# A two-layer graph network on one core: three more products of the second half cut into an inner seven, and the order of the work around them changed

## The chip, the cores and the metric

The kernel runs on one core of a Trainium2 chip. The metric is the device time of one execution, in microseconds (us). The engines named are PE (TensorE, the matrix multiplier, with PEld for its weight loads), DVE (VectorE), ACT (ScalarE), POOL (GpSimd) and SP (which issues transfers). Matmuls write to PSUM[...]; the other engines take results out of the banks ("evict" below) to SBUF. POOL doesn't read PSUM here: it adds and subtracts blocks that lie in SBUF.

## What is computed

The reference, cut to what matters. `x` is 16 x 1024 x 64, `adj` is 1024 x 1024, all in float32.

```python
# layer 0, attention over the nodes, then a residual and a layernorm
score = softmax(einsum('bnc,bmc->bnm', Q, K), axis=1)
out = einsum('bnm,bmc->bnc', einsum('bnm,mc->bnc', score, adj), V)
x = layernorm(x + out)
# layer 1, two hops over the graph (both supports are adj), then a residual and a layernorm
x1 = adj @ x0;  x2 = 2.0 * (adj @ x1) - x0        # twice, with the same adj
out = concatenate([x0, x1, x2, x1, x2], -1) @ weight + bias
x = layernorm(x + out)
```

The kernel applies the weights before the hops, so that layer 1 becomes a chain of products of `adj` with a 1024 x 1024 matrix (nodes by 8 pairs of batches with 2 x 64 channels each): first z = B + adj · Y, then the output = X + adj · z. Y, B and X are three mixtures of x0.

## The kernel before, in words

Nodes lie on the partitions: a tile [128, 8, 1024] holds a 1024 x 1024 matrix. `aT` holds adj transposed, `UY` holds Y, `XB` holds B and then z, `xs` holds X and then the output. Columns are ordered by pair p = 0 to 7; the "second half" is pairs 4 to 7, columns 512 to 1023.

Every large product is done as Strassen-Winograd's seven products over 2 x 2 blocks. `SIDE[1..7]` are the seven left operands: four blocks of adj (1, 2, 4, 7; `SIDE[1]` and `SIDE[2]` lie in `aT` itself) and three sums of blocks (3, 5, 6, in `S`). The right operands are four blocks and four sums of blocks. Each product is added to one to three of the four result blocks (`TO`): 1 and 2 to 00, 5 and 7 to 11, 6 to 01, 10 and 11, 4 to 10, 3 to 01. In the order `STEPS` = 1, 2, 7, 5, 6, 4, 3 the products 6, 4 and 3 are accumulated in PSUM on top of the bank that still holds 1, 7 and 5 (`CHAIN`). So 6 can't start before 1 has been evicted, 4 not before 7, and 3 not before 5.

A main loop over the eight pairs does attention; products of the first layers fill the gaps of PE. Its last matmul ends 430.43 us into the span. Behind it stands the tail, which is written out by hand: the order in the program is the order on each engine, and the change is made there. The tail does the rest of z's second half, then the product adj · z with an inner seven in each of its seven products (`one` to `seven`), then the last layernorm and the stores.

A product of z's second half has a left operand of 512 x 512 and a right one of 512 x 256. It can be done in two ways:

- direct, in two steps g = 0 and 1 (`z_step(n, g)`), each of 8 matmuls of 256 columns (16 instructions, since one float32 matmul is recorded as two), one bank, and DVE adds of 128x512 to each place it goes to, at L658;
- by an inner seven (`Inner`, `of_z(n, sa, tb)`): the product is cut again. Four sums of blocks of the left side (`of_a`, into `sa`, 128x512 each) and four of the right side (`of_b`, into `tb`, 128x256 each) are made at L727, by POOL unless DVE is named. The seven steps have 4 matmuls of 128 columns each (8 instructions), and their evictions are 128x256. Step 7 needs `sa[2]` and `tb[2]`, step 5 `sa[0]` and `tb[0]`, step 6 `sa[1]` and `tb[1]`, step 4 `tb[3]`, step 3 `sa[3]`. Steps 1 and 2 need no sums.

Before the change, products 3 and 4 of z's second half (called z3 and z4 here) have an inner seven; 1, 2, 5, 6 and 7 are direct. The four sums of the right operands at the outer level, 128x1024 each, are made by DVE at L238 (`hop_z.sums(k)`): sums(1) makes operand 5, sums(2) operand 6, sums(3) operand 7, sums(4) operand 4.

The last pair, q = 7, also ends its attention in the tail: `values` (PE), adds on DVE, `squared` (ACT), `spread` (DVE, and a power on POOL, L424), `normed` and a transpose (DVE), two transfers to turn the layout (SP), a copy into order on ACT (`x0T_in_order`), and then `mix(q, kk)` for kk = 0, 2, 4, 6: PE makes two nodes' rows of the three mixtures in two banks, ACT evicts Y and B (L465, L466), then DVE evicts X (L470). `mix(6, kk)` are the last of pair 6. `added(U, 0, 0)` are two transfers issued on POOL's queue that add U, a result of `one`, to `xs`; they wait for `one`'s last evictions. What POOL has to do later is queued behind them.

The sums need scratch. Tiles are taken by tag (`xT`, `GT`, `o`, `t`, `oT`, `u`, `e`), and a new tile of a tag waits until the old one's readers are done. z3's and z4's left sums lie before the change in V (the second result tile of `one`'s kind) and in tiles `xT`.

Of the kernel before, what the change touches and what calls it, by code (L numbers as in the profile page):

```python
# [11 lines left out]
ALU = mybir.AluOpType  # L12
# [14 lines left out]
def gnn_kernel(  # L27
# [156 lines left out]
    def quarter(big_tile, h, r, c):  # L184

        t = big_tile[:, K4 * r : K4 * (r + 1), h * H + c * Q : h * H + (c + 1) * Q]
        return t.rearrange("p k (q f) -> p q k f", q=2)
# [97 lines left out]
    def xT(p):  # L285
        if p not in XT:
            XT[p] = att.tile([P, N], FP, tag="xT", name="xT")
        return XT[p]
# [243 lines left out]
    y = [[quarter(UY, 0, r, c) for c in range(2)] for r in range(2)]  # L532
    hop_z = Hop(lambda r, c: y[r][c], into(XB, 0), (y[0][1], y[1][1], y[0][0], y[1][0]), u, THIRD)
    runs = []
    for hop, orders in (
        (hop_0, (((6, 7), ONE), ((5, 3), ONE))),
        (hop_1, (((1, 2), ONE), ((6, 7, 4), ONE), ((5, 3), ONE))),
        (hop_z, (((1, 2), ONE), ((5, 3), ONE), ((6, 7, 4), ONE))),
    ):
        runs += [(hop, n, g) for order, groups in orders for g in groups for n in order]  # L540
    more = {(0, 1), (0, 3), (HP + 1, 3), (HP + 2, 3), (NP - 1, 2), (NP - 1, 3)}


    ahead, behind_all = {}, {
        (0, 0): [lambda: transposed(1, xT(1))], (0, 3): [value_weights], (0, 4): [mix_weights],
        (1, 0): [lambda: hop_1.sums(1)], (1, 5): [lambda: hop_1.sums(2)],
        (2, 0): [lambda: hop_1.sums(4)],
        (HP + 2, 5): [lambda: hop_z.sums(2)], (HP + 2, 6): [lambda: hop_z.sums(3)],
        (HP + 2, 7): [lambda: hop_z.sums(4)],
    }  # L550
    ahead.update({
        (0, 1): [lambda: sums_of_adj(1)], (0, 2): [lambda: sums_of_adj(4)],
        (2, 0): [lambda: hop_1.sums(3)], (HP + 1, 4): [lambda: hop_z.sums(1)],
    })

    def later(step, do, p):
        behind_all.setdefault(step, []).append(lambda: do(p))

    for p in range(NP):
        later((p, 4 if p else 5), means, p)  # L560
        later((p, 6) if p != HP + 2 else (p + 1, 0), centre, p)
        if p + 1 < NP:
            later((p + 1, 1), spread, p)
            later((p + 1, 2), normed, p)
            later((p + 1, 3), x0T, p)
        if p + 2 < NP:
            later((p, 7), lambda p: transposed(p, xT(p)), p + 2)
    mix_of = {(p, m): (p - 1, 2 * (m - 5)) for p in range(1, NP) for m in (5, 6, 7)}
    mix_of.update({(p, 1): (p - 2, K8 - 2) for p in range(2, NP)})

    for m in (6, 7):
        del mix_of[NP - 1, m]

    def run():

        hop, n, group = runs.pop(0)
        po = f_tile(f"p{n}")
        hop.product(po, n, group, True)
        return lambda: hop.evict(po, n, group)

    late, late_too = [run() for _ in range(2)], []
    for p in range(NP):
        q = p - 1
        for m in range(K8):
            nxt = (p, m + 1) if m + 1 < K8 else (p + 1, 0)
            if nxt[0] < NP:
                sc = scores(*nxt)
            scaled(p, m)
            for evict in late:
                evict()  # L590
            late = []
            for do in ahead.get((p, m), ()):
                do()
            if m == 1 and p:
                squared(q)
            if m == 5 and p:
                x0T_in_order(q)
            behind = late_too + [run()]
            late_too = []
            weighted(p, m)  # L600
            if nxt[0] < NP:
                exps(*nxt, sc)
            for evict in behind:
                evict()
            for do in behind_all.get((p, m), ()):
                do()
            if m == K8 - 1:
                attended(p)
            if (p, m) in more:
                (late_too if m == 1 else late).append(run())  # L610
            if m == 0 and p:
                late += values(q)
            if m == 2 and p + 1 < NP:
                late.append(project(p + 1))
            if (p, m) in mix_of:
                late += mix(*mix_of[p, m])
    assert not runs

    for evict in late:
        evict()
# [4 lines left out]
    q = NP - 1  # L629
    for_pool, for_vector = [], []  # L630

    def behind(pool=2, vector=1):

        for _ in range(min(vector, len(for_vector))):
            for_vector.pop(0)()
        for _ in range(min(pool, len(for_pool))):
            for_pool.pop(0)()
# [25 lines left out]
    hop_z = Hop(lambda r, c: y1[r][c], None, t, None, None)  # L663
# [4 lines left out]
    def z_step(n, g, **kw):  # L668
        step(
            held[CHAIN.get(n, n), g], n, SIDE[n][:, :, ts(g, 2 * P)], hop_z.side[n],  # L670
            lambda r, c: d_z(r, c, (2 * g, 2 * g + 1)), to=TO_Z,
        )
        behind(**kw)
# [68 lines left out]
    def of_z(n, sa, tb):  # L742

        return Inner(n, lambda r, c: hop_z.side[n][:, c, 2 * r : 2 * r + 2], sa, tb)
# [6 lines left out]

    def own(c):

        t = [att.tile([P, 2, K4, P], FP, tag="e", name=f"own{c}", bufs=4) for c in range(2)]
        return t, lambda r, c: t[c][:, :, 2 * r : 2 * r + 2].rearrange("p q g f -> p g q f")
# [75 lines left out]
    X, Y = ("xT", "xT", "GT", "GT"), ("o", "t", "oT", "u")  # L831
    one = of_full(1, X)
    (a3, a2, a1, a4), of_b = one.of_a, one.of_b
    for_vector += one.sums((a3, *of_b[:3], a2, a1, of_b[3], a4), nc.vector)
    for evict in mix(q - 1, 2):
        evict()
    z_step(2, 0, vector=2)
    for evict in values(q, w[1:3]):
        evict()
    squared(q)  # L840
    z_step(1, 0, vector=2)
    for evict in mix(q - 1, K8 - 4):
        evict()
    spread(q)
    z_step(2, 1, vector=2)
    for evict in mix(q - 1, K8 - 2):
        evict()
    normed(q)
    x0T(q)
    for do in for_vector:  # L850
        do()
    for_vector.clear()
    U, d_u = own(0)
    for i, n in enumerate(STEPS):
        one.step(n, w, d_u, True)
        behind()
        if i == 4:
            x0T_in_order(q)
    for kk, banks in (0, None), (2, (w[1], w[0])):
        for evict in mix(q, kk, banks):  # L860
            evict()
    hop_z.sums(1)

    V, d_v = own(1)
    t = [v.rearrange("p q k f -> p (q k f)") for v in V]
    z3 = of_z(
        3, blocks_of(t, Q),
        [SIDE[1][:, k, 0:Q].rearrange("p (k f) -> p k f", k=2) for k in range(K4)],
    )
    t = tiles(*X[:3])  # L870
    z4 = of_z(4, blocks_of(t[:2], Q), blocks_of(t[2:], P))
    for do in added(U, 0, 0) + z3.sums(z3.of_a) + z4.sums(z4.of_a):
        do()
    z_step(1, 1)
    for evict in mix(q, K8 - 4):
        evict()
    z_step(5, 0)
    for evict in mix(q, K8 - 2):
        evict()
    hop_z.sums(2)  # L880
    z_step(5, 1)
    hop_z.sums(3, 4)
    two = of_full(2, Y)
    for do in (
        z3.sums(z3.of_b) + z4.sums(z4.of_b) + two.sums(two.of_a) + two.sums(two.of_b)
    ):
        do()
    for g in range(2):
        for n in (6, 7):
            z_step(n, g)  # L890


    turn = [f_tile(f"w{i}") for i in (4, 5)] + [w[i] for i in (1, 0, 3, 2)]
# [6 lines left out]
    for z_n, d in (z3, in_z(0, 1)), (z4, in_z(1, 0)):  # L900
        b4 = next_banks(4)
        for n in STEPS:
            z_n.step(n, b4, d)


    five = of_full(5, X)
# [3 lines left out]
    for i, n in enumerate(STEPS):  # L910
        two.step(n, b4, in_x(0, 0))
        behind()
        if i == 1:
            (a3, a2, a1, a4), of_b = five.of_a, five.of_b
            for do in five.sums((a3, *of_b[:3], a2, a1, of_b[3], a4)):
                do()
    six = of_full(6, Y)
# [4 lines left out]
    for i, n in enumerate(STEPS):  # L922
        five.step(n, b4, d_v, True)
        behind()
        if i in (0, 2, 4):
            (norm.square, norm.variance, norm.out)[i // 2]()
    seven = of_full(7, X)
# [3 lines left out]
    for n in STEPS:  # L931
        six.step(n, b4, d_u)
        behind()
# [5 lines left out]
    for i, n in enumerate(STEPS):  # L939
        seven.step(n, b4, d_w, True)  # L940
        if i == 1:
            for_pool += added(V, 1, 1) + added(V, 0, 1)
        behind(4)
        if i in (0, 2, 4):
            (norm.square, norm.variance, norm.out)[i // 2]()
# [90 lines left out]
```

## Time and profile before

| | us |
|---|---|
| median of three runs | 582.42 (582.37 to 583.14) |
| the profiled execution, whole | 582.48 |
| its span, from first to last instruction | 580.6 |
| first matmul of the tail | at 430.43 |
| z's second half done (first step of `two`) | at 497.69 |
| `seven` done (first of the wide steps, L951) | at 546.12 |

| window (us) | PE busy | DVE busy | ACT busy | POOL busy |
|---|---|---|---|---|
| 430 to 440 | 10.00 | 3.89 | 2.76 | 0.00 |
| 440 to 450 | 10.00 | 9.11 | 2.16 | 2.90 |
| 450 to 460 | 10.00 | 4.70 | 4.18 | 2.94 |
| 460 to 470 | 10.00 | 6.15 | 1.57 | 9.69 |
| 470 to 480 | 10.00 | 8.35 | 0.00 | 9.69 |
| 480 to 490 | 10.00 | 4.93 | 0.00 | 9.67 |
| 490 to 500 | 10.00 | 5.61 | 0.00 | 1.27 |

A row of the second table gives the time in which each engine had an instruction under way. In a timeline line of the profile the numbers are the start, the time until the group's last end, the engine, the line of the program, the operation, the tile written and those read, the shape, and the count; in brackets stands the idle time before it and what ended it. Durations of neighbours overlap by some 0.05 to 0.1 us, so the distance between two starts is used where one follows another.

### The profile page before, as it was taken

Reading aid. Unit: us, or ns where it says so; the run is one execution under the profiler, and the core shown is the slowest. Engines: PE = TensorE matmul, PEld = TensorE weight load, DVE = VectorE, ACT = ScalarE, POOL = GpSimd, SP = SyncE. Lnnn points to the kernel's source line nnn. Section 1 sums busy time; section 2 is a strip of 40 time slices with the busy share of each in tenths; the row PEclk is TensorE's granted clock in tenths of the full one; section 3 lists DMA queues with packets and bytes.
Section 4 is the critical chain, followed back from the end, with each engine's and each line's share of the span. In section 5 each row is a group of like instructions: output and inputs, shape, how many; then the busy total and the mean of one; then the engine's idle time right before and its main releaser. Section 6 shows DMA issues by size and latency. Waiting matters only on the chain.

```text
span 580.6 us, 9494 instructions
## 1 busy us (share of the span) xinstructions
PE 571.9 (99%) x3774; PEld 328.7 (57%) x3774; DVE 441.1 (76%) x725; ACT 243.9 (42%) x517; POOL 113.9 (20%) x75
## 2 busy tenths in 40 slices
PE   8999999999999999999999999999999999999995
PEld 7754545444444444444444454444458889988744
DVE  0788878878867887787787777888858575689776
ACT  1134344556546545555554544554532300023471
POOL 0000002000200100100010010001001497494785
PEclk9999999999999999999999999999999999999999
DMA  8901001202022020211202011000200600001955
GB/s 258 337 21 53 1 26 49 72 1 74 1 73 73 2 73 2 73 40 35 73 1 73 37 37 71 4 1 2 72 1 1 146 0 2 2 0 37 173 134 164
DMA packets 26350, 33.35 MB, mean 57 GB/s; under 512 B 3010, under 2 KB 19650, under 8 KB 25922
## 3 DMA queue, kind: packets, MB, share of 16 engines
q1 hardware_dynamic: 24130, 28.55, 14.7%
q0 software_dynamic: 2176, 4.19, 4.0%
q8 instruction: 30, 0.49, 0.4%
q14 instruction: 14, 0.11, 0.1%
HBM read 16.48 MB, written 12.06 MB: 49 GB/s over the span
## 4 chain that ended last, share of the span: by engine, by line
PE 95%; DVE 1%; DMA 1%; SPq 1%; ACT 1%; POOL 0%; issue 0%; POOLq 0%; ACTq 0%
PE p L246 23%; PE sc L354 21%; PE acc L390 19%; PE w L643 16%; PE pm L455 5%; PE w L951 3%; PE wide L643 2%; PE pq L323 1%; PE po L407 1%; PE pv L246 1%; PE pu L246 1%; DMA early<-in_wqT_dram 1%; SPq L91 0%; DVE xs L799 0%; DVE var L421 0%; ACT xs L805 0%
## 5 line engine op out<-in xcount | busy, mean ns | idle before, releaser
L368 ACT ACTIVATE e<-sc,nm 128x1024 f32<-128x1024 f32 x128 | 142.7, 1115 | 150.8 <-DVE nm L366 150.8
L366 DVE TENSOR_REDUCE nm<-sc 128x1 f32<-128x1024 f32 x128 | 150.7, 1219 | 43.1 <-PE sc L354 42.9
L424 POOL TENSOR_TENSOR rstd<-var,expo 128x16 f32<-128x16 f32 (+3 forms) x21 | 50.7, 2420 | 429.9 <-DVE ri L376 377.1
L354 PE MATMUL sc<-xT,GT 64*128 64x512 f32 x512 | 126.8, 605 | 0.0
L390 PE MATMUL acc<-e,us 128*64 128x512 f32 x512 | 120.7, 592 | 0.0
L354 PEld LDWEIGHTS sc<-xT,GT 64*128 64x128 f32 x512 | 51.6, 186 | 49.2 <-issue 37.7
L390 PEld LDWEIGHTS acc<-e,us 128*64 128x64 f32 x512 | 36.7, 137 | 45.8 <-issue 36.6
L470 DVE TENSOR_TENSOR xs<-pm,bias 128x128 f32<-128x128 f32 x62 | 17.8, 290 | 19.3 <-ACT XB L466 17.8
L455 PEld LDWEIGHTS pm<-w,x0T_k 64*128 64x128 f32 x248 | 19.4, 186 | 22.8 <-DVE UY L267 6.5
L246 PE MATMUL p<-XB,S 128*64 128x256 f32 x256 | 31.1, 385 | 0.0
L246 PE MATMUL p<-UY,aT 128*64 128x256 f32 x256 | 31.0, 384 | 0.0
L465 ACT ACTIVATE UY<-pm 128x128 f32<-128x128 f32 x62 | 17.4, 281 | 28.9 <-PE pm L455 28.9
L455 PE MATMUL pm<-w,x0T_k 64*128 64x192 f32 x248 | 28.5, 349 | 0.0
L246 PEld LDWEIGHTS p<-XB,S 128*64 128x64 f32 x256 | 17.0, 136 | 18.9 <-issue 6.6
L246 PEld LDWEIGHTS p<-UY,aT 128*64 128x64 f32 x256 | 17.3, 137 | 18.3 <-DVE xs L470 5.3
L656 ACT COPY own<-w 128x512 f32<-128x512 f32 x8 | 4.5, 588 | 54.7 <-PE w L643 54.7
L368 ACT ACTIVATION_READ_ACCUMULATOR e<-sc,nm 128x1 f32 x128 | 24.7, 193 | 0.0
L658 DVE TENSOR_TENSOR XB<-w,XB 128x256 f32<-128x256 f32 (+1 forms) x28 | 13.5, 516 | 13.3 <-PE w L643 13.3
L246 PE MATMUL p<-UY,S 128*64 128x256 f32 x192 | 23.3, 385 | 0.0
L246 PE MATMUL p<-XB,aT 128*64 128x256 f32 x192 | 23.3, 384 | 0.0
L246 PEld LDWEIGHTS p<-UY,S 128*64 128x64 f32 x192 | 12.8, 136 | 14.1 <-DVE xs L470 3.0
L378 DVE TENSOR_TENSOR us<-UY,ri 128x128 f32<-128x128 f32 x64 | 19.1, 298 | 2.2
(191 smaller groups left out, 811.5 us busy)
## 6 DMA issues: line engine op xcount, KB each, us to landing
d<-blocks SPq DMA_DIRECT2D x15, 512.0 KB, 2.6
x0T<-d SPq DMA_DIRECT2D x32, 128.0 KB, 2.8
xs<-own POOLq DMA_DIRECT2D x8, 512.0 KB, 6.4
xT<-d SPq DMA_DIRECT2D x28, 128.0 KB, 2.8
out_dram<-xs SPq DMA_DIRECT2D x14, 256.0 KB, 2.7
xs<-in_x_dram SPq DMA_DIRECT2D x3, 1024.0 KB, 7.3
aT<-in_adjT_dram SPq DMA_DIRECT2D x8, 256.0 KB, 5.4
aT<-in_adjT_dram SPq DMA_DIRECT2D x4, 512.0 KB, 7.8
```

Of the source, the lines that this page charges most:

```text
L246: nc.tensor.matmul(po[t * w : (t + 1) * w], SIDE[n][:, k, j : j + w], self.side[n][:, :, k, :], start=start, stop=True, skip_group_check=True,
L354: nc.tensor.matmul(sc[j][:, ts(h, H)], GT[p][half[j], ts(m, P)], xT(p)[half[j], ts(h, H)], start=True, stop=True,)
L366: nc.vector.tensor_reduce(nm, sc[j], AX.X, ALU.max, negate=True)
L368: nc.scalar.activation(e, sc[j], AF.Exp, bias=nm, accum_out=sm[:, j : j + 1])
L378: nc.vector.tensor_tensor(us, UY[:, m, ts(p, P)].rearrange("p (j c) -> p j c", j=2), ri[:, :, None].to_broadcast([P, 2, C]), ALU.mult,)
L390: nc.tensor.matmul(ACC[p][half[j], ts(h, H)], us[:, j], es[j][:, ts(h, H)], start=(m == 0), stop=(m == K8 - 1),)
L424: nc.gpsimd.tensor_tensor(rstd, var, expo[:, 0:n], ALU.pow)
L455: nc.tensor.matmul(pm[j][:, 0:3, k], X0T[p][half[j], ts(kk + k, P)], w3[half[j]], start=True, stop=True,)
L465: nc.scalar.activation(part(UY, j), pm[j][:, 0], AF.Copy)
L470: nc.vector.tensor_tensor(xs[:, p, kk : kk + 2, half[j]], pm[j][:, 2], bias[:, None, :].to_broadcast([P, 2, C]), ALU.add,)
L643: nc.tensor.matmul(po[:, ts(g, b.shape[1] * P)], a[:, k, ts(g, P)], b[:, :, k, :], start=start and g == 0 and k == 0, stop=True, skip_grou ...
L951: nc.tensor.matmul(po, SIDE[n][:, k, ts(i, P)], B_F[n][:, k, cols], start=k == 0, stop=k == K4 - 1)
```

## The change

Products 2, 5 and 7 of z's second half get an inner seven as well (`z2`, `z5`, `z7`); 1 and 6 stay direct.

- z2's sums are put on POOL inside the main loop, in the last pair's round m = 2. Its steps are the first of the tail, and add to z's block 00.
- z5 and z7, whose products go to two blocks each, collect their result in a tile of their own (`t5` in tag `u`, `t7` in tag `o`), with four of the nine places of a seven written by ACT copies and five by DVE adds; then DVE adds the whole tile (128x1024) to each of its two blocks (`add_z`). t5 is added between z7's steps, t7 between z3's.
- The right-hand sums of z5 and z7 are made by DVE, all other sums of z's products by POOL. `one`'s left sums move from DVE to POOL.
- `one`, the first product of the output, stands after z2 and z_step(1, 0); `normed` and the transposition of the last pair stand before `mix(6, 6)`; the copy into order on ACT moves from behind the fifth of `one`'s steps to behind the third.
- `two`'s left sums stand on POOL before those of z7, and its right sums before those of z4. Scratch tags are handed round anew.

Much of the diff moves definitions ahead of the main loop and renames (`hop_z` to `hop_z1`, `behind` to `follow`); that is left out here.

```diff
+    def flat(t):
+        t = t.rearrange("p (k f) -> p k f", k=K4)
+        def d(r, c):
+            return t[:, 2 * r : 2 * r + 2, ts(c, P)].rearrange("p g (q f) -> p g q f", q=1)
+        return t, d
+    def add_z(t, r, c):
+        z = XB[:, K4 * r : K4 * (r + 1), H + Q * c : H + Q * (c + 1)]
+        nc.vector.tensor_tensor(z, t, z, ALU.add)
...
+    def z2_sums():
+        t = XB[:, :, H + 3 * P :]
+        z2.append(of_z(
+            2, blocks_of(tiles("xT", "GT"), Q), [t[:, 2 * i : 2 * i + 2] for i in range(4)]
+        ))
+        for do in z2[0].sums(z2[0].of_a + z2[0].of_b):
+            do()
+    behind_all.setdefault((NP - 1, 2), []).append(z2_sums)
...
+    do_all(mix(q - 1, 2))
+    for i, n in enumerate(STEPS):
+        z2[0].step(n, w, in_z(0, 0))
+        if i == 1:
+            do_all(values(q))
+            squared(q)
+        elif i == 4:
+            spread(q)
     one = of_full(1, X)
-    for_vector += one.sums((a3, *of_b[:3], a2, a1, of_b[3], a4), nc.vector)
...
-    z_step(2, 0, vector=2)
...
-    z_step(1, 0, vector=2)
...
-    z_step(2, 1, vector=2)
...
+    do_all(one.sums(one.of_a))
+    do_all(mix(q - 1, K8 - 4))
+    do_all(one.sums(one.of_b, nc.vector))
+    z_step(1, 0)
     normed(q)
     x0T(q)
+    do_all(mix(q - 1, K8 - 2))
     U, d_u = own(0)
+    V, d_v = own(1)
+    v_flat = blocks_of([v.rearrange("p q k f -> p (q k f)") for v in V], Q)
+    z5 = of_z(5, v_flat, blocks_of(tiles("t"), P))
+    do_all(z5.sums(z5.of_a))
     for i, n in enumerate(STEPS):
         one.step(n, w, d_u, True)
-        if i == 4:
+        if i == 2:
             x0T_in_order(q)
     for kk, banks in (0, None), (2, (w[1], w[0])):
+        do_all(mix(q, kk, banks))
+    hop_z1.sums(1)
+    do_all(z5.sums(z5.of_b, nc.vector))
+    two = of_full(2, X)
+    do_all(added(U, 0, 0) + two.sums(two.of_a))
     z_step(1, 1)
-    z_step(5, 0)
...
-    z_step(5, 1)
-    hop_z.sums(3, 4)
...
+    do_all(mix(q, K8 - 4))
+    w_flat = [SIDE[1][:, 2 * k : 2 * k + 2, ts(j, Q)] for k in range(2) for j in range(2)]
+    z7 = of_z(7, w_flat, blocks_of(tiles("oT"), P))
+    do_all(z7.sums(z7.of_a))
+    t5, d5 = flat(tiles("u")[0])
+    for i, n in enumerate(STEPS):
+        z5.step(n, w, d5, True)
+        if i == 3:
+            do_all(mix(q, K8 - 2))
+            hop_z1.sums(2)
+    hop_z1.sums(3)
+    do_all(z7.sums(z7.of_b, nc.vector))
+    z3 = of_z(3, v_flat, blocks_of(tiles("t"), P))
+    do_all(z3.sums(z3.of_a) + z3.sums(z3.of_b) + two.sums(two.of_b))
+    z_step(6, 0)
+    hop_z1.sums(4)
+    t7, d7 = flat(tiles("o")[0])
+    for i, n in enumerate(STEPS):
+        z7.step(n, w, d7, True)
+        if i in (1, 3):
+            add_z(t5, *((0, 1), (1, 1))[i // 2])
+    z4 = of_z(4, w_flat, blocks_of(tiles("oT"), P))
+    do_all(z4.sums(z4.of_a) + z4.sums(z4.of_b))
+    z_step(6, 1)
-    for g in range(2):
-        for n in (6, 7):
-            z_step(n, g)
...
+    b4 = next_banks(4)
+    for i, n in enumerate(STEPS):
+        z3.step(n, b4, in_z(0, 1))
+        if i in (1, 3):
+            add_z(t7, *((1, 0), (1, 1))[i // 2])
+    b4 = next_banks(4)
+    for n in STEPS:
+        z4.step(n, b4, in_z(1, 0))
```

## The prediction

> **What bounds the kernel now.** I read the page first: busy shares and the chain that ended last.
>
> ```profile
> PE 571.9 (99%) x3774; PEld 328.7 (57%) x3774; DVE 441.1 (76%) x725; ACT 243.9 (42%) x517; POOL 113.9 (20%) x75
> ...
> PE 95%; DVE 1%; DMA 1%; SPq 1%; ACT 1%; POOL 0%; issue 0%; POOLq 0%; ACTq 0%
> ```
>
> PE is the bound, and no wait of it is on the chain in the tail: whatever shortens PE's work there shortens the kernel, unless PE begins to wait. Second, PE's timeline, for what the two kinds of product cost.
>
> ```profile
> 463.31 3.72 PE L643 MATMUL w<-UY,S 128*128 128x256 f32 x16
> ...
> 478.28 3.62 PE L643 MATMUL wide<-UY,S 128*128 128x256 f32 x16
> 481.73 3.62 PE L643 MATMUL w<-UY,aT 128*128 128x256 f32 x16
> 485.19 1.95 PE L643 MATMUL w<-UY,S 128*128 128x128 f32 x16
> ...
> 491.44 1.95 PE L643 MATMUL w<-UY,aT 128*128 128x128 f32 x16
> ...
> 497.69 3.62 PE L643 MATMUL w<-XB,aT 128*128 128x256 f32 x16
> ```
>
> A direct step takes 481.73 - 478.28 = 3.45 us, or 3.65 behind the 64-row matmuls of mix (463.31 to 466.96). An inner seven takes 6.25 us (485.19, 491.44, 497.69): 0.893 for each step. Third, POOL's timeline in that stage, because the new sums go there.
>
> ```profile
> 468.38 1.26 POOL L727 TENSOR_TENSOR in_xT<-in_xT,aT 128x512 f32<-128x512 f32 x1
> 469.61 2.25 POOL L727 TENSOR_TENSOR in_xT<-aT,in_xT 128x512 f32<-128x512 f32 x1
> ...
> 473.43 1.59 POOL L727 TENSOR_TENSOR aT<-aT,UY 128x256 f32<-128x256 f32 x1
> 474.98 1.70 POOL L727 TENSOR_TENSOR aT<-UY,aT 128x256 f32<-128x256 f32 x1
> 476.65 0.72 POOL L727 TENSOR_TENSOR in_GT<-UY 128x256 f32<-128x256 f32 x1
> ...
> 488.72 1.27 POOL L727 TENSOR_TENSOR in_u<-XB,in_oT 128x512 f32<-128x512 f32 x1
> ```
>
> POOL has no gap from 459 to 490. A sum costs it 1.27 (512 wide) or 0.73 (256 wide), but a few cost about 1 more. Fourth, DVE's timeline at those moments.
>
> ```profile
> 468.94 1.79 DVE L238 TENSOR_TENSOR UY<-UY 128x1024 f32<-128x1024 f32 x1
> ...
> 472.78 3.32 DVE L238 TENSOR_TENSOR UY<-UY 128x1024 f32<-128x1024 f32 x2
> ...
> 500.23 1.22 DVE L692 TENSOR_TENSOR UY<-XB 128x1024 f32<-128x1024 f32 x1
> ```
>
> The same shape takes 1.22 with POOL idle (500.23), and 1.79 or 1.66 with POOL busy. The first, asked for at 468.94, ends 1.09 after POOL's sum has ended at 469.64; POOL's next, begun at 469.61, ends 1.13 after DVE's end at 470.73. Then two sums of DVE and two of POOL take turns. Whoever comes second waits for the whole instruction.
>
> **What the Trainium skill says.** "SBUF — State Buffer", section "Who interferes with whom": a DVE instruction with two SBUF inputs contends with a GpSimd instruction that reads SBUF, by an exclusive lock for the whole instruction; one with at most one SBUF input doesn't. The trace agrees: the lines above, and the PSUM evictions at L658, which stay at 0.69 beside a busy POOL. "TensorE: Matmul & The Clock Gate", section "Back-to-back issue gap": at few columns the weight load sets the spacing too. It agrees: 893/8 = 112 ns an instruction at 128 columns, 216 at 256, so halving saves little more than the eighth fewer products. "PSUM — Partial Sum Buffer", section "PSUM bank collisions raise a hardware error": engines are kept apart by bank. In this program DVE waits 2.1 us for ACT's own-copy (L656) before it reads the same bank.
>
> **The change part by part.** All clock times below are a timetable on the old trace's clock: PE's tail begins at 430.43, and z's second half ended at 497.69.
>
> PE's work. Removed: six direct steps, 3.65 + 3.66 + 3.65 + 3.56 + 3.46 + 3.46 = 21.44 (from the starts of PE's timeline, 431.28 to 485.19). Added: 3 x 6.25 = 18.75, and 0.2 for each restart behind 64-row work (3.65 - 3.45): z2 behind mix and behind `values`, z5 twice behind mix, 0.8. Sum -1.89: without waits z ends at 495.8.
>
> z2's eight sums in the main loop. POOL is idle there from 398.77 (a power) to 443.61. They need 4 x 1.27 + 4 x 0.73 = 8 us from 398.8, so they end near 408; PE needs them from 433. They delay DVE's two-input sums there (normed at 400.07, L378 at 401.39, L267 at 402.93 and 407.09) by up to 1.2 each; DVE waits 0.8, 1.0 and 1.15 for PE in this stretch, and takes that up. Nothing, at worst 1: at 415.1 the scores follow the exp at once.
>
> `one`'s sums. POOL can begin when z2's step 6 (437.2) and the power of `spread` (442.7) are done; `one` needs its first sum at 448.0, two PE steps after 444.4. Hidden, as DVE's four right sums are, though their last waits for one of POOL's.
>
> The copy into order on ACT. z_step(1, 0) ends at 443.5; DVE's last right sum (behind POOL's first, to 444.7), the step's add 0.6, `normed` behind POOL's second (445.8 to 446.9) and the transposition 1.17 follow. It ends at 448.0 (449.1 before), the copy began 7.04 after it (449.11 to 456.15), so at 455.1, and ends at 456.1. It now stands in front of ACT's two copies for product 6 on ACT. Those end at 457.1, DVE's last three adds of `one` 1.9 later, at 459.0 (before: 458.1, though `one` ends 0.65 earlier now). Costs: mix(q, 2) takes banks w[0] and w[1], PE waits 0.3 for the first of the three; and `added(U)`, and all of POOL's queue behind it, begins late: 460.9 (459.6 before).
>
> POOL from there to z4. In order: `two` left, z7 left, z3 left, z3 right, `two` right, z4 left, z4 right. Four left sums take 5.16 (479.62 to 484.78), as `two`'s right ones do, four narrow ones 2.97 (476.65 to 479.62). Up to the third of z4's right sums, which step 7 needs: 5 x 5.16 + 2.97 + 2.3 = 31.1. DVE takes turns with it. The price of a wide one is measured: the first sixteen sums took 459.65 to 479.62 = 19.97 instead of 2 x 5.16 + 2 x 2.97 = 16.26, with four of DVE's: 0.93 each. In the new stretch fall seven (sums 2, 3 and 4; four `add_z`, of which no row exists: two SBUF inputs of 128x1024 as in L692, 1.22): 6.5. Of z5's and z7's right sums there are eight; nearest row L267 XB<-u,XB 128x256, 0.43. Each costs POOL between 0 and 0.34; I take 0.13, as POOL's own start-up then lies in the wait: 1.0. So 460.9 + 31.1 + 7.5 = 499.5. PE could use that sum at 495.8 - 5 x 0.893 = 491.3. It can't: steps 7, 5, 6, 4, 3 follow from 499.6, z ends at 504.1. Nothing shortens that but fewer turns: before, z3's and z4's sixteen sums came first on POOL, ahead of `two`'s.
>
> DVE on the way. It loses in the same turns, up to 1.13 for each small sum. From 472.7: sum 3 (1.1), z7's four right sums each behind one of POOL's 1.13 (4 x 1.42), z_step(6, 0)'s three adds (1.8), sums(4) (0.35 + 1.08), product 2's add 0.34, add_z 0.24 + 1.08, and product 5's add, at 484.8. z7's step 3 is on top of 5's bank; PE stands there from 481.7. By that timetable PE waits 0.3 before mix(q, 2), 0.3 for z5's right sums, 0.7 for mix(q, 6)'s bank, 0.1 for sums(2), 1.1 for z7's step 7, 3.1 for its step 3, 0.8 at z3's step 4: 6.4 before z4, and 1.7 more at z4's step 7, where POOL is late. The ACT copies of 128x256 have no row, they lie between 0.28 (128x128) and 0.59 (128x512); I took 0.33, and nobody waits for one by itself.
>
> Behind z. `two`'s sums are done; `five`'s find POOL free at z's end, as before, where POOL waited for PE until 496.15 and for DVE until 501.52. The rest keeps its order and its lengths, so what z loses the end loses: 504.1 - 497.7 = +6.4. The profiled execution took 582.48, of which the span is 580.6 and 1.88 lies around it: 588.9, and since the median is 582.42, 588.8 for the median.
>
> **The rivals.**
>
> - A: only one of the two queues is late. If POOL's sums come in time (its start at 459.6 and no turns lost to narrow sums, say) but DVE's don't, z ends at 495.8 + 6.4 = 502.2: 587.0. If the turns cost DVE half (two of POOL's in a row can't be excluded, only wide pairs are seen), 2 to 4 us of waits less: 584 to 586. For it: the narrow turns are inferred. Against: either queue is enough.
> - B, the other side: the lock hardly decides, because POOL's sums fall between DVE's. Then POOL has its last needed sum at 460.9 + 31.1 = 492.0, 0.7 after 491.3, and with POOL's queue begun 1 us earlier none is left: -1.9, 580.6. It decides from a loss below some 2 us of the 7.5. Against it: four of four wide sums in the old trace met POOL busy.
> - C: gain and waits cancel, within 0.2% (1.16 us), which is about what a measurement here can tell from no change: waits of 0.7 to 3.1 in all. Nothing singles this out.
> - That it doesn't do what it says: PE's records would show no 128-wide steps before `one`. The diff leaves no room for it.
> - Upwards: the copy into order later by 1 or 2 (its transfers took 7), or PE's clock. "TensorE: Matmul & The Clock Gate", section "Why this matters for your kernels", warns that idle gaps over about 3 us take the clock down; the trace of before has none (granted clock 0.998), mine has one of 3.1. Either adds 1 to 3: up to 592.
>
> **How the numbers follow.** Both queues late, +4 to +9: 0.62, with the upward cases. A: 0.18. C: 0.08. B: 0.12. The time is the first case's, 588.8. The likeliest's own range is 586.5 to 592; down to 583.5 it takes in A and leaves out C and B. Faster 0.12, same 0.08, slower 0.80.
>
> **What would show it.** Right: POOL without a gap from about 461 to 500, sums of 1.6 to 2.3 at each two-input sum of DVE; z7's right sums on DVE at 1 to 1.6 instead of 0.43; PE idle at z7's steps 7 and 3 and at z4's step 7, released by DVE and POOL; 6.25 for z2; z's end at 503 to 506; everything behind it shifted by one amount. Wrong: POOL done with z4's right sums by 492; narrow sums of DVE at 0.43 beside a busy POOL; a wait in the main loop after 398; or a later part that takes the loss back.

## The result, and the profile after

The changed kernel takes 592.76 us (median of five runs, 592.16 to 593.46) against 582.42 before: a ratio of 1.0174, 95% interval 1.0162 to 1.0185, some 10 us slower. The forecast was slower, 588.8, with a range to 592.0; the time lies 0.8 above it. The profiled execution has a span of 591.0 (580.6 before).

First the page of the changed kernel: busy shares, the granted clock of PE in 40 slices, and the chain that ended last.

```profile
PE 575.5 (97%) x3846; PEld 333.3 (56%) x3846; DVE 460.5 (78%) x742; ACT 246.6 (42%) x525; POOL 143.3 (24%) x95
...
PEclk9999999999999999999999999999999997999999
...
PE 87%; DVE 6%; DMA 2%; issue 1%; ACT 1%; SPq 1%; POOL 0%; POOLq 0%; DVEq 0%; ACTq 0%
```

PE had 95% of the chain and has 87%; DVE has come onto it with 6%. One slice of the clock shows a 7. Now the timeline of PE in the changed kernel, where z's second half is made (start, time, operation; in brackets what ended the idle time before).

```profile
430.46 0.92 PE L455 MATMUL pm<-w,x0T_k 64*128 64x192 f32 x8
...
458.26 0.91 PE L455 MATMUL w<-w,x0T_k 64*128 64x192 f32 x6 [0.34 <-DVE own L564]
...
464.27 2.02 PE L549 MATMUL w<-UY,S 128*128 128x128 f32 x16 [0.60 <-ACT XB L466]
468.48 2.02 PE L549 MATMUL w<-in_t,own 128*128 128x128 f32 x16 [2.19 <-DVE in_t L633]
...
481.11 3.81 PE L549 MATMUL w<-in_oT,aT 128*128 128x128 f32 x32 [1.02 <-DVE in_oT L633]
487.68 2.04 PE L549 MATMUL w<-UY,aT 128*128 128x128 f32 x8 [2.76 <-DVE in_o L564]
489.52 5.78 PE L549 MATMUL wide<-UY,S 128*128 128x256 f32 x16
495.13 1.95 PE L549 MATMUL w<-UY,S 128*128 128x128 f32 x16
...
508.08 3.62 PE L549 MATMUL w<-XB,aT 128*128 128x256 f32 x16
```

The tail begins as before (430.46 against 430.43), and z is done at 508.08 against 497.69: 10.39 later, which is the whole loss (the spans differ by 10.4). The forecast had PE's work shorter by 1.9, so waits and clock together cost some 12. PE waits five times for DVE or ACT up to 487.68, most at z5's step 7 (2.19) and at z7's step 3 (2.76). Then something else: z_step(6, 1) takes from 489.52 to 495.13, 5.61, where a direct step took 3.45. The windows of PE show why (length, PE busy, granted clock, DMA).

```profile
484.00:485.00 1.00, 0.92 (x9) 1.00 0.00 0
485.00:486.00 1.00, 0.00 (x0) 1.00 0.00 0
486.00:487.00 1.00, 0.00 (x0) 1.00 0.00 0
487.00:488.00 1.00, 0.32 (x1) 0.53 0.00 0
488.00:489.00 1.00, 1.00 (x6) 0.50 0.06 16
...
492.00:494.00 2.00, 2.00 (x6) 0.53 0.00 0
494.00:495.00 1.00, 1.00 (x6) 1.00 0.00 0
```

After the gap the clock is halved for some 7 us. z7's step 3 takes 1.84 instead of 0.89 and z_step(6, 1) 2.16 more: 3.1 lost. DVE in the changed kernel, at the sums and adds that PE waited for:

```profile
460.11 4.02 DVE L238 TENSOR_TENSOR UY<-UY 128x1024 f32<-128x1024 f32 x1
464.16 1.37 DVE L633 TENSOR_TENSOR in_t<-UY 128x256 f32<-128x256 f32 x1
...
476.77 1.37 DVE L633 TENSOR_TENSOR in_oT<-UY 128x256 f32<-128x256 f32 x1
...
485.25 1.95 DVE L663 TENSOR_TENSOR XB<-in_u,XB 128x1024 f32<-128x1024 f32 x1
487.12 0.41 DVE L564 TENSOR_TENSOR in_o<-w,in_o 128x256 f32<-128x256 f32 x1
487.46 1.95 DVE L663 TENSOR_TENSOR XB<-in_u,XB 128x1024 f32<-128x1024 f32 x1
```

Sums from SBUF beside a busy POOL are long, 1.37 for 256 columns and 1.95 for 1024; an add from PSUM (487.12), 256 columns too, takes 0.41. The line at 460.11 is the surprise: 4.02 for a sum that took between 1.22 and 2.06 in the kernel before. POOL at that moment and at the end of its queue for z:

```profile
459.12 2.61 POOL L791 DMA_DIRECT2D xs<-own  x2 [4.52 <-DVE own L564]
460.79 2.24 POOL L633 TENSOR_TENSOR in_xT<-aT 128x512 f32<-128x512 f32 x1
463.11 2.14 POOL L633 TENSOR_TENSOR in_xT<-aT,in_xT 128x512 f32<-128x512 f32 x1
...
498.48 1.58 POOL L633 TENSOR_TENSOR in_oT<-in_oT,UY 128x256 f32<-128x256 f32 x1
500.03 0.72 POOL L633 TENSOR_TENSOR in_oT<-UY,in_oT 128x256 f32<-128x256 f32 x1
```

When DVE's sums(1) comes (460.11), POOL is writing out the two transfers of U (until 461.73), and one of its sums is next (until 463.03). DVE ends 1.1 after that, at 464.13. So the 4.02 are 1.62 until the transfers are out, 1.30 for POOL's sum and 1.10 for its own work. And z4's third right sum is done at 498.48 + 1.58 = 500.06, while PE reaches the step that needs it at 503.6: POOL isn't what PE waits for there.

### The profile page after: what moved, and what is told of

Same layout as the page of the kernel before. It is cut to its first block, busy times and chain, and to the rows that moved or that the text cites. A ratio compares the mean times of both kernels' runs of the same rounds, so it can differ in the third digit from the quotient of the medians.

```text
span 591.0 us, 9701 instructions
## 1 busy us (share of the span) xinstructions
PE 575.5 (97%) x3846; PEld 333.3 (56%) x3846; DVE 460.5 (78%) x742; ACT 246.6 (42%) x525; POOL 143.3 (24%) x95
## 4 chain that ended last, share of the span: by engine, by line
PE 87%; DVE 6%; DMA 2%; issue 1%; ACT 1%; SPq 1%; POOL 0%; POOLq 0%; DVEq 0%; ACTq 0%
PE p L246 23%; PE sc L354 20%; PE acc L390 19%; PE w L549 12%; PE pm L455 4%; PE w L982 2%; PE wide L549 2%; PE po L407 1%; PE pq L323 1%; DVE UY L238 1%; PE pv L246 1%; PE pu L246 1%; DMA early<-in_wqT_dram 1%; DVE XB L564 1%; DVE in_t L633 1%
## 5 line engine op out<-in xcount | busy, mean ns | idle before, releaser
L246 PEld LDWEIGHTS p<-XB,aT 128*64 128x64 f32 x192 | 12.9, 137 | 13.5 <-issue 3.6
```

The costliest lines, as they stand in the source:

```text
L246: nc.tensor.matmul(po[t * w : (t + 1) * w], SIDE[n][:, k, j : j + w], self.side[n][:, :, k, :], start=start, stop=True, skip_group_check=True,
```

## The experiments

All compare with the kernel before on the same chip; times are medians. The diffs are against the changed kernel unless said otherwise, and `...` marks lines left out.

**Product 2 alone.** From the kernel before: z2 and the new order of the first stage, the copy on ACT in its old place, 5 and 7 direct.

```diff
+    for i, n in enumerate(STEPS):
+        z2[0].step(n, w, in_z(0, 0))
...
-    z_step(2, 0, vector=2)
-    z_step(2, 1, vector=2)
```

> Product 2 alone gets the inner seven; 5 and 7 stay direct, POOL's and DVE's work from sums(1) on is that of before, and the copy into order on ACT stands behind the fifth step of `one` as before. My theory (the loss comes from DVE and POOL taking turns at the sums of z5 and z7, not from an inner seven as such): PE saves 3.65 + 3.66 - 6.25 - 0.4 = 0.66, no wait of PE appears, 581.8, ratio 0.9988. Rival (an inner seven at 128 columns saves PE nothing, or the eight sums on POOL in the main loop hold up the attention): 582.4 to 583.5.

Measured: 582.05 against 582.95, ratio 0.9984 (0.9977 to 0.9992), and no wait of PE in the tail. The ratio forecast, 0.9988, lies within the interval: an inner seven gains what PE's rows say, and the eight sums in the main loop cost nothing that shows. So the loss comes from what this run leaves out: z5 and z7, the order of POOL's and DVE's work around them, and the copy's new place.

**Work in the gap.**

```diff
+    spare = f_tile("spare")
     for i, n in enumerate(STEPS):
+        if i == 6:
+            for _ in range(12):
+                nc.tensor.matmul(spare[:, 0:P], ident, ident, start=True, stop=True)
         z7.step(n, w, d7, True)
```

> The changed kernel with 12 small matmuls into a spare bank put in front of z7's step 3, so that PE works (some 2.7 us) where it was idle for 2.8. They add work and leave all waits as they are. My theory (after the gap PE's clock was halved from 487 to 494, which cost 3.1): the clock stays at 1.0, z_step(6, 1) takes 3.45 instead of 5.6, and the end comes 2.5 to 3.1 earlier, 589.7 to 590.3; no more than that, since POOL's sums for z4 (ready at 500.1) are the next to wait for. Rival (the low clock has another cause, or the time at the end is set by POOL all the same): 592 to 593.

Measured: 590.80, ratio 1.0132 (1.0118 to 1.0146), against 1.0174 without. PE's timeline of this kernel:

```profile
484.23 2.84 PE L915 MATMUL spare<-ident 128*128 128x128 f32 x24
487.17 1.13 PE L549 MATMUL w<-UY,aT 128*128 128x128 f32 x8
488.13 3.62 PE L549 MATMUL wide<-UY,S 128*128 128x256 f32 x16
...
500.72 3.84 PE L549 MATMUL w<-in_oT,aT 128*128 128x128 f32 x32 [0.17 <-POOL in_oT L633]
```

More work, less time: z_step(6, 1) is back at 3.46 (488.13 to the next start at 491.59), and the kernel is about 2.4 faster by the ratios. Then PE waits 0.17 for POOL, at z4's step 7: POOL's sums are the next wall, as expected, so not all of the 3.1 comes back. The gap itself is filled here, not removed.

**Transfers of U behind the left sums of `two`.**

```diff
-    do_all(added(U, 0, 0) + two.sums(two.of_a))
+    do_all(two.sums(two.of_a) + added(U, 0, 0))
```

> The changed kernel with the two transfers of U to xs issued on POOL behind the four left sums of `two` instead of ahead of them. My theory (while POOL writes out these transfers, DVE's sums(1) with two SBUF inputs can't start: it took 4.0 instead of 1.1 to 1.9): sums(1) takes under 2.4, z5's step 1 and step 7 wait 1.5 to 2 less, and the end comes 1 to 5 earlier depending on whether the gap at z7's step 3 still halves the clock: 588 to 591.5. Rival (sums(1) is long because of POOL's sums alone, taking turns): sums(1) stays over 3 and the time at 592 to 593.

Measured: 590.53, ratio 1.0131 (1.0116 to 1.0145). DVE's timeline:

```profile
460.22 1.71 DVE L238 TENSOR_TENSOR UY<-UY 128x1024 f32<-128x1024 f32 x1
461.97 3.01 DVE L633 TENSOR_TENSOR in_t<-UY 128x256 f32<-128x256 f32 x1
465.01 1.38 DVE L633 TENSOR_TENSOR in_t<-UY,in_t 128x256 f32<-128x256 f32 x1
```

sums(1) takes 1.71, but the next sum, only 256 wide, takes 3.01. POOL writes its transfers out from 460.78 to 463.38 in this run, and its next sum starts at 462.45, after DVE had asked at 461.97. What holds DVE off moves with the transfers, so it isn't a sum that stood ahead of it. Both sums have two inputs from SBUF. The wait at z5's step 7 stayed at 2.17; step 1's went.

**Transfers of U behind z4's sums.** The same edit, but with `added` at the end of z4's sums; the order of what stands ahead of sums(1) on DVE stays as it is.

```diff
-    do_all(added(U, 0, 0) + two.sums(two.of_a))
+    do_all(two.sums(two.of_a))
...
-    do_all(z4.sums(z4.of_a) + z4.sums(z4.of_b))
+    do_all(z4.sums(z4.of_a) + z4.sums(z4.of_b) + added(U, 0, 0))
```

> The changed kernel with the transfers of U issued behind z4's sums; the copy on ACT stays early, so `one`'s last adds stay late. My theory (writing out the transfers keeps DVE's two-input sums off): sums(1) falls from 4.0 to 2.1 or less though nothing before it moved, z5's step 7 waits some 1.0 instead of 2.2, POOL's sums come 1 to 2.6 earlier, and the end 2.5 to 4.5 earlier, 588 to 590. Rival (the late adds of `one` alone cost it, not the transfers): sums(1) stays near 4, 591.5 to 593.

Measured: 589.05, ratio 1.0108 (1.0095 to 1.0122).

```profile
461.35 1.48 DVE L238 TENSOR_TENSOR UY<-UY 128x1024 f32<-128x1024 f32 x1
462.87 1.37 DVE L633 TENSOR_TENSOR in_t<-UY 128x256 f32<-128x256 f32 x1
```

The tail of this run begins 1.0 later in its profile, and counted from that, DVE's last adds of `one` end no earlier than in the changed kernel. sums(1) takes 1.48 all the same, PE's wait at z5's step 7 is 0.30, less than expected. The gap at z7's step 3 is 3.18, and the clock still falls there, for a shorter time (see the next run).

**The copy on ACT back in its place.**

```diff
-        if i == 2:
+        if i == 4:
             x0T_in_order(q)
```

> The changed kernel with the copy into order on ACT behind the fifth of `one`'s steps, where it stood before. My theory (it delays ACT's copies for product 6, DVE's last adds of `one` and with them the transfers of U, which then fall on sums(1)): the wait of 0.34 at mix(q, 2) goes, the transfers start about 1 earlier, sums(1) takes 1 to 2 less than 4.0, and the end comes 0.5 to 2 earlier, 590.5 to 592. Rival (a harmless move): 592.5 to 593.

Measured: 588.42, ratio 1.0102 (1.0083 to 1.0121): twice what I expected, 4.2 by the ratios. `one`'s last adds end sooner, the transfers are written out from 456.44 to 459.36, just ahead of sums(1):

```profile
459.70 2.05 DVE L238 TENSOR_TENSOR UY<-UY 128x1024 f32<-128x1024 f32 x1
461.79 1.37 DVE L633 TENSOR_TENSOR in_t<-UY 128x256 f32<-128x256 f32 x1
```

The waits at mix(q, 2) and at z5's step 1 are gone, and the one at its step 7 is 1.02. One line of ACT's order costs 4.2, by way of DVE's adds, POOL's queue and DVE's first sum. Part of that is the clock, as PE's timeline of this run shows:

```profile
485.32 1.68 PE L549 MATMUL w<-UY,aT 128*128 128x128 f32 x8 [2.75 <-DVE in_o L564]
486.79 4.78 PE L549 MATMUL wide<-UY,S 128*128 128x256 f32 x16
491.41 1.95 PE L549 MATMUL w<-UY,S 128*128 128x128 f32 x16
```

Behind the same gap, 2.75, step 3 and z_step(6, 1) take 1.47 and 4.62, so the low clock costs 1.75 here and 3.1 in the changed kernel's profile. The two runs with the transfers moved lose 1.74 and 1.76. What makes the low clock last longer in the one than in the others, no run shows.

**Both: the copy back, and work in the gap.** The two edits shown above, together.

> The changed kernel with both: the copy into order on ACT where it was before, and 12 small matmuls (added work) in the gap at z7's step 3. What is left is the turns of DVE and POOL at z7 and z4. My theory: the two effects add up, less what POOL's sums for z4 then hold: 586 to 587.5. Rival (one of the two took the other's place): 588 to 589, as with the copy alone.

Measured: 587.98, ratio 1.0088 (1.0073 to 1.0104), above what I expected, at the rival's figure, and not told apart from the copy alone (1.0102, 1.0083 to 1.0121). The two gains don't add up: the clock holds, but PE again waits 0.17 for POOL at z4's step 7, which starts at 498.8. Without either effect the change still costs some 5: waits for DVE of 1.0 at z5 and again at z7, the gap at z7's step 3, filled but still there, and POOL's sums for z4, which end last.

**DVE's work moved away from z7's step 3.** sums(4) and both adds of t5 behind z7's steps.

```diff
     z_step(6, 0)
-    hop_z1.sums(4)
...
         z7.step(n, w, d7, True)
-        if i in (1, 3):
-            add_z(t5, *((0, 1), (1, 1))[i // 2])
+    hop_z1.sums(4)
+    for r in range(2):
+        add_z(t5, r, 1)
```

> The changed kernel with sums(4) and the two adds of t5 to z moved behind z7's steps on DVE, so that product 5 of z7 is evicted ahead of them. My theory (z7's step 3 waits 2.8 for that eviction, which stands behind 1.45 + 0.4 + 1.95 us of DVE's work, and the clock falls in the gap): the wait goes, the clock stays at 1.0, and z7's step 3 starts 2.8 earlier; the end is then held by POOL's sums for z4, near 588.5 to 590. Rival (the wait at step 3 is set by something else, the ACT copies or the sums of z7): step 3 starts at 487 to 488 as before and the time stays at 592 to 593.

Measured: 592.97, ratio 1.0174 (1.0158 to 1.0189), no gain. The wait at step 3 did go, as my theory said, but PE met DVE's work again in z3 (PE's timeline):

```profile
495.39 1.16 PE L549 MATMUL w<-in_t,own 128*128 128x128 f32 x8 [1.33 <-DVE XB L564]
498.58 1.13 PE L549 MATMUL w<-in_t,S 128*128 128x128 f32 x8 [2.04 <-DVE XB L564]
```

The clock fell behind these gaps (0.50 from 500 to 502). I had named the right wait and the wrong worth: the work that takes turns was only moved, and PE met it later.

**The left sums of `two` moved behind z4's.**

```diff
-    do_all(added(U, 0, 0) + two.sums(two.of_a))
+    do_all(added(U, 0, 0))
...
-    do_all(z4.sums(z4.of_a) + z4.sums(z4.of_b))
+    do_all(z4.sums(z4.of_a) + z4.sums(z4.of_b) + two.sums(two.of_a))
```

> The changed kernel with the four left sums of `two` moved on POOL from ahead of z7's sums to behind z4's. POOL's amount of work is the same. My theory (each of DVE's small right sums waits for one of POOL's 1.1 to 1.2 sums, so it takes 1.37 instead of 0.42, and PE at z5's step 7 waits for the third): POOL is idle until z_step(1, 1) ends at 462.8, so one or two of z5's right sums take 0.42, z5's step 7 starts 1 to 2.5 earlier, and the end comes 1.5 to 4 earlier, 588.5 to 591. Rival (narrow sums are slow by themselves, or PE's wait is for something else): the four stay at 1.37 and the time at 592 to 593.

Measured: 592.12, ratio 1.0154 (1.0139 to 1.0170), not told apart from the changed kernel. It didn't make the idle POOL that it was meant to: z7's sums moved up at once behind the transfers (460.82), and the first three right sums of z5 stayed at 1.37. The fourth, at 468.29, took 0.41: POOL's sums had ended at 468.08, and its next began at 470.33. So a narrow sum isn't slow by itself. The clock fell twice in the profile, once behind the gap of 2.19 that the changed kernel has too and passed at full clock.

**All three, with POOL's sums by need.** POOL: z7's left sums, transfers, z3, z4, then `two`; t5 added behind z7, t7 within z4; the copy on ACT in its old place. No work is added or taken away.

```diff
-        if i == 2:
+        if i == 4:
             x0T_in_order(q)
...
-    do_all(added(U, 0, 0) + two.sums(two.of_a))
...
-    do_all(z7.sums(z7.of_a))
+    do_all(z7.sums(z7.of_a) + added(U, 0, 0))
...
-    do_all(z3.sums(z3.of_a) + z3.sums(z3.of_b) + two.sums(two.of_b))
+    do_all(z3.sums(z3.of_a) + z3.sums(z3.of_b))
...
-        if i in (1, 3):
-            add_z(t5, *((0, 1), (1, 1))[i // 2])
+    for r in range(2):
+        add_z(t5, r, 1)
...
-    do_all(z4.sums(z4.of_a) + z4.sums(z4.of_b))
+    do_all(z4.sums(z4.of_a) + z4.sums(z4.of_b) + two.sums(two.of_a) + two.sums(two.of_b))
...
```

> All three products with an inner seven, as in the changed kernel, but POOL's sums in the order in which PE needs them (z7, transfers of U, z3, z4, then `two`), the adds of t5 and t7 behind z7's steps and within z4's, and the copy on ACT where it was before. The work of each engine is that of the changed kernel. My theory (order, not amount, makes most of the loss): 583 to 587, with the clock at 1.0. Rival (DVE and POOL together have too much two-input work between 457 and 500 whatever the order): 589 to 593.

Measured: 584.59, ratio 1.0031 (1.0020 to 1.0043), the clock at 1.0 from 456 to 505. Of the loss some 8.3, by the ratios, were order. What is left are waits of PE for DVE, above all 1.31 at z7's step 3 and 0.68 at z4's step 4. Its DVE also shows a right sum with POOL idle and busy side by side (POOL's next sum begins at 461.04), and an add from PSUM in the midst of the transfers (465.22 to 467.82, POOL's line below).

```profile
460.90 0.42 DVE L633 TENSOR_TENSOR in_t<-UY,in_t 128x256 f32<-128x256 f32 x1
461.36 1.37 DVE L633 TENSOR_TENSOR in_t<-in_t,UY 128x256 f32<-128x256 f32 x1
...
466.49 0.42 DVE L564 TENSOR_TENSOR in_u<-w,in_u 128x256 f32<-128x256 f32 x1 [1.02 <-PE w L549]
```

```profile
465.22 2.60 POOL L791 DMA_DIRECT2D xs<-own  x2
```

**Products 2 and 5, 7 direct.** On POOL z4's left sums, the transfers, z3's sums, z4's right ones, `two`'s; the copy on ACT in its old place. Only the added lines are shown.

```diff
+    do_all(z4.sums(z4.of_a) + added(U, 0, 0))
...
+    do_all(z3.sums(z3.of_a) + z3.sums(z3.of_b))
     z_step(6, 0)
+    hop_z1.sums(3, 4)
+    do_all(z4.sums(z4.of_b) + two.sums(two.of_a) + two.sums(two.of_b))
+    z_step(7, 0)
     z_step(6, 1)
+    add_z(t5, 0, 1)
+    z_step(7, 1)
+    add_z(t5, 1, 1)
```

> Products 2 and 5 with an inner seven, 7 direct; the copy on ACT where it was before; on POOL z4's left sums first, then the transfers of U, z3's sums, z4's right sums and those of `two`, each where its operands come free. My theory (an inner seven gains 0.6 if DVE and POOL don't meet on what PE waits for): 580.8 to 582.5, at or below the kernel with z2 alone (582.05). Rival (two-place collection costs more than the seven gains, through DVE's adds of 128x1024): 583 to 586.

Measured: 588.20, ratio 1.0091 (1.0077 to 1.0105). That was neither theory: I had put sums(3) behind z_step(6, 0)'s adds, z_step(7, 0) waited 3.35 for it, and ran at half clock after that (5.25 from its start at 478.38 to the next at 483.63). Mended, against the run above:

```diff
-    z_step(6, 0)
-    hop_z1.sums(3, 4)
+    hop_z1.sums(3)
+    z_step(6, 0)
+    hop_z1.sums(4)
```

> As e7_z2_z5, but sums(3) stands on DVE ahead of z_step(6, 0)'s adds, as in the changed kernel, and not behind them (in e7 z_step(7, 0) waited 3.35 for it and the clock fell). My theory (the wait of e7 was of my own making; an inner seven for 2 and 5 gains 1.2 on PE and two adds of 128x1024 fit on DVE): no wait over 0.3, 581 to 582.5. Rival (collection of two places costs more than it gains even so): 583 or more.

Measured: 581.92 against 582.74, ratio 0.9987 (0.9981 to 0.9994), one wait of 0.18. It is some 0.8 faster than the kernel before, and not told apart from product 2 alone (0.9984), so no gain of the inner seven for product 5 shows. The place of one sum on DVE was worth some 6 us between these two runs.

## Why the prediction was right and wrong

- The main loop, PE's work and `one`: right. The tail begins 0.03 later, z2 with its two restarts takes 439.05 - 431.31 - 1.09 = 6.65 as summed, `one` starts at 444.40 without a wait. One remark on it was off: 6.25 against 2 x 3.45 saves 9%, less than the eighth, and 112 ns is only 4 above half of 216, so the lines hardly show a floor set by the weight load.
- The lock between DVE's sums from SBUF and POOL's: right. A narrow sum goes from 0.42 to 1.37 (I had 1.42), and z7's step 7 waits 1.02 (1.1). "SBUF — State Buffer", section "Who interferes with whom", states it for two-input instructions, and the runs agree, narrow ones included. That z7's step 3 waits 2.76 (I had 3.1) is in part luck: PE came to it 3.2 later than in my timetable, and the add that it needs came 2.7 later.
- POOL's third right sum of z4: 500.06, where I had 499.5. But PE didn't wait for it in the changed kernel, although I had said that it would.
- What z loses the end loses: right, 10.39 and 10.4.
- Wrong, the step that failed: the copy into order on ACT and the transfers of U behind it. I let the late copy cost PE 0.3 at mix(q, 2), and the late transfers a later start of POOL's queue (459.6 to 460.9). The transfers' effect on DVE I put at nothing: sums(1) isn't among the seven wide sums that I charged a turn. It took 4.02: while POOL writes transfers out, a DVE sum with two SBUF inputs doesn't start, and POOL's next sum then went first. The trace of before had the two just apart, with the transfers out at 459.63 (POOL's line, then DVE's):

```profile
458.42 1.21 POOL L767 DMA_DIRECT2D xs<-own  x1 [0.35 <-PE pm L455]
```

```profile
459.96 2.06 DVE L238 TENSOR_TENSOR UY<-UY 128x1024 f32<-128x1024 f32 x1
```

So PE waits 2.19 at z5's step 7, where I had 0.3 for z5's right sums, product 5 of z7 is added at 487.5 instead of 484.8, and z7's step 3 is 2.85 late. Moving the transfers (1.0108) or the copy (1.0102) takes about 4 off, of which some 1.3 is the shorter time at the low clock in those profiles.

- Mis-sized: PE's clock. I had the gap of about 3 and the page that warns of it ("TensorE: Matmul & The Clock Gate", section "Why this matters for your kernels"), but kept it as an upward case of 1 to 3 beside the forecast. It cost 3.1 in the profile. The forecast contained the gap, so it should have contained the clock. The page's limit of about 3 us is also too wide for this kernel: the clock fell behind 2.76 here and behind 2.19 in the run with `two`'s left sums moved.
- The sum of the miss: 2.85 + 3.1, less the waits that a late PE no longer meets (0.21 instead of 0.8 in z3, none instead of 1.7 at z4's step 7), is 3.7 of the 4.0 between 10.4 and 6.4. With either of the two out of the way the time lies below 592: 590.80 with the clock held, 589.05 or 588.42 with the transfers away from sums(1).
- The rivals: B, no lock, is out, and so is C, no change. A, one queue late, fails by its time (z at 502.2; it was 508.08). It is right in that PE waited for DVE and ACT in the changed kernel and never for POOL; that POOL is late too shows only in the two runs with matmuls in the gap, by 0.17. Whether the clock falls at a given gap I can't say beforehand: it held after 2.17 to 2.20 in four profiles, the changed kernel's among them, and fell after 2.19 in that of the run with `two`'s left sums moved.

## What to carry to other kernels

Count the work of two engines that take turns at one resource as one queue, up to the moment at which its last result is needed: here the sums, adds and transfers that the change put ahead of z4's last sum. POOL's part alone, 31 us as the prediction summed it, with DVE's and the transfers stood before a step that PE could have reached some 30 us after POOL's queue began; in the order of need `two`'s 10 us of it stood behind that step, and most of the loss was gone. An order that puts early what is needed late cost some 8 us here with no work added, and a move on an engine that nobody waits for (ACT's copy) can cost 4 us two queues away. And a forecast that opens a gap on PE of over 2 us has to price the half clock that may follow it.

## What the hardware showed that I had not expected

Issuing transfers from POOL keeps DVE's two-input sums from SBUF off, for as long as they are written out: 4.02 for a sum that takes 1.48 with the transfers elsewhere, and 3.01 for one that takes 0.42 with POOL idle and 1.37 beside POOL's sums. An add from PSUM beside such transfers keeps its 0.42 (the run with POOL's sums by need). PE's clock fell to half after gaps of 2.2 to 3.4 us, and once behind two of 1.3 and 2.0 close together, for about 3.5 to 7 us; filling a gap of 2.8 with useless matmuls made the kernel 2.4 us faster.
